# Query, key and value projections: Strassen in float32 replaced by three float32r passes over exact digits

## Chip, cores and metric

The kernel runs on one core of one Trainium2 chip. The metric is device time in microseconds (us) from the first to the last instruction of the core, as the median of several executions of the same program. Engines are named as the profile names them: PE (TensorE, matmuls), PEld (its weight loads), DVE (VectorE), ACT (ScalarE), POOL (GpSimd) and SP (SyncE, which here only issues transfers).

## What is computed

Four sequences of 512 tokens with 1024 features, all in float32. Layer norm, then causal attention with 16 heads and rotary positions, then a gated layer whose weights are signs and whose in- and out-scales are mixed by a router over eight experts; the two are multiplied and added to the input.

```python
x = hidden_states                                  # (4, 512, 1024)
xn = layernorm(x)
q, k, v = xn @ Wq, xn @ Wk, xn @ Wv                # each 1024 x 1024, 16 heads of 64
q, k = rotary(q), rotary(k)
attn = softmax(causal(q @ k.T) / 8)
s = (attn @ v) @ Wo
routing = softmax(xn @ gate_w.T)                   # 8 experts
o = ((xn * (routing @ in_scale)) @ sign(weight).T) * (routing @ out_scale) + bias
out = x + s * silu(o)
```

## The kernel before

**Stages.** The main part goes through the four sequences ("batches") in turn. A batch has four groups of heads; one group is two units, and a unit is two heads (128 rows of Q and K). `projections(b)` is a generator that yields after each matmul of Q, K and V. `interleave` draws from it between the pieces of the attention of the group before, so that TensorE always has a projection matmul to do while softmax runs elsewhere. Then a tail does the last attention, the gated layer and the output projection for eight pairs of token tiles. TensorE's order is the program's order; the other engines are ordered by a scheduler from the data they depend on, but for calls that are pinned. Every engine and every transfer queue runs its own list in order.

**Projections (lines 249 to 498).** `keys` lists ten weight sets a batch: query and key of four groups, and values of two groups at a time. Each set is a 2x2 block product and is done by Strassen with seven products instead of eight: `project_qk` and `project_v` multiply sums of weight quarters (`form_w`, on DVE) with sums of quarters of the normalized, transposed input (`form_x`, on DVE), all in float32 with 256 columns a matmul (L338 for Q and K, L425 for V). V comes out with tokens on the partitions, Q and K with features there. Results are put together by ACT (copies out of the accumulators), DVE (L352, L389, L451) and POOL (L388, L478). `load_w` fetches the next weights, 1 MB a transfer, on SP's queue, into three buffers. `rotary` takes four copies on ACT, one operation on DVE and two on POOL for each unit of Q and K.

**Input.** `load_x`, `half_statistics`, `deviation` and `normalize` do the layer norm of a tile of 128 tokens; `transpose_x` turns it on TensorE (L200) and copies it to `X[b]` on ACT or DVE; the turned tile also goes to device memory (`xn_d`) for the tail. At the start, before the first group, the four tiles of batch 0 go through this one after the other, with projection matmuls between them.

**Router (L629).** `router(b, 0)` multiplies the 32 padded columns of the gate weights with all four token tiles: for each of eight chunks, four matmuls go to four different column groups of the array. Later steps do the softmax over experts.

**Attention.** `scores` (L525), `softmax` (DVE maxima and masks, ACT exponentials with sums, POOL scaling at L561), `transpose_blocks` (ten block transposes on DVE, then 16 moves of 80 KB on SP's queue, L589), `values` (L604, with a copy on ACT and a transfer to `at_d`).

**Around it.** `load_sign` and `make_sign` make the sign weights in four of the groups, from staging tiles of the pool `xin`. `load_scales` and `split_scales` do the same for the expert scales. In batch 3 the first pairs of the tail are prepared on the score banks: `in_scales(0)`, `in_scales(1)` and `out_scales(0)`. The tail's two-part products of the gated layer (`ffn`, L1011, and `gated_by_strassen`, L1180) already use float32r operands: each activation is split into a high and a low part, the signs are exact.

Of the kernel before, what the change touches and what calls it, by code (L numbers as in the profile page):

```python
# [35 lines left out]

# [6 lines left out]
def attn_gated_ffn_kernel(  # L43
# [3 lines left out]
    wqk: bass.AP,  # L47
    wv: bass.AP,
# [16 lines left out]
    sgp = ctx.enter_context(tc.tile_pool(name="sign", bufs=1))  # L65
# [48 lines left out]
    rt_d = dp.tile([B, TPB, 32, P], F32, name="rt_d")  # L114

    sg = {n: sgp.tile([P, E], F32R, name=f"sg{n}") for n in range(NC - 1)}
# [5 lines left out]
    xip = ctx.enter_context(tc.tile_pool(name="xin", bufs=2))  # L122
# [14 lines left out]
    fp = left(name="forms", bufs=1)  # L137
# [14 lines left out]
    X, xin = {}, {}  # L152

    X1 = xp.tile([P, TPB, E], F32, tag="X", name="x_0")

    def load_x(b, t):
        if b == 0:
            xt = X1[:, t, :]
        else:
            xt = xip.tile([P, E], F32, tag="x", name=f"x_{b}_{t}")  # L160
        nc.sync.dma_start(out=xt, in_=x[(b * TPB + t) * P : (b * TPB + t + 1) * P, :])
        xin[b, t] = xt
# [30 lines left out]

    def transpose_x(b, t, g):
        if b not in X:
            X[b] = xp.tile([P, NC, S], F32, tag="X", name=f"X_{b}")
        tp = tp_bank(f"xtp_{b}_{t}_{g}")
        for j in range(4):
            c = 4 * g + j
            nc.tensor.transpose(tp[:, j, :], xin[b, t][:, c * P : (c + 1) * P], ident)  # L200
        dst = X[b][:, 4 * g : 4 * g + 4, t * P : (t + 1) * P]

        if (g == 0 and b > 0) or (g == 1 and (b, t) == (0, TPB - 1)):
            nc.vector.tensor_copy(dst, tp)
        else:
            nc.scalar.copy(dst, tp)
        if g == 1:

            queue = nc.scalar if (b, t) == (B - 1, TPB - 1) else nc.sync
            queue.dma_start(  # L210
                out=xn_d[b, t].rearrange("p (c q) -> p c q", c=NC),
                in_=X[b][:, :, t * P : (t + 1) * P],
            )


    W, Q, K, V = {}, {}, {}, {}
    groups = [(b, g) for b in range(B) for g in range(NGRP)]


    keys = [  # L220
        (b, g, m)
        for b in range(B)
        for g, m in ((0, 0), (0, 1), (1, 0), (1, 1), (0, 2), (2, 0), (2, 1), (3, 0), (3, 1), (2, 2))
    ]

    def load_half_w(key, i):
        if i == 0:
            W[key] = wp.tile([P, 2, NC, P], F32, tag="w", name="w_%d_%d_%d" % key)
        nc.sync.dma_start(
            out=W[key][:, i].rearrange("p c n -> p (c n)"),  # L230
            in_=wqk[key[1], key[2]][:, i * E : (i + 1) * E],
        )


    waiting = [(key, i) for key in keys for i in range(2) if key[2] == 2 or i == 0]

    def load_w():

        if not waiting:
            return  # L240
        key, i = waiting.pop(0)
        b, g, m = key
        if m < 2:
            W[key] = wp.tile([P, 2, NC, P], F32, tag="w", name=f"w_{b}_{g}_{m}")
            nc.sync.dma_start(out=W[key].rearrange("p i c n -> p (i c n)"), in_=wqk[g, m])
        else:
            W[key, i] = wp.tile([P, NC, 2 * P], F32, tag="w", name=f"w_{b}_{g}_{m}_{i}")
            nc.sync.dma_start(
                out=W[key, i].rearrange("p c n -> p (c n)"), in_=wv[g // 2, i]
            )  # L250

    SF, TF = {}, {}

    def quarters_w(key):
        if key[2] < 2:
            w = W[key]
            return w[:, 0, :4, :], w[:, 0, 4:, :], w[:, 1, :4, :], w[:, 1, 4:, :]  # L260
        w, v = W[key, 0], W[key, 1]
        return w[:, :4, :], w[:, 4:, :], v[:, :4, :], v[:, 4:, :]

    def quarters_x(b):
        t = X[b]
        return t[:, :4, :TH], t[:, :4, TH:], t[:, 4:, :TH], t[:, 4:, TH:]

    def form_w(key, n):
        a11, a12, a21, a22 = quarters_w(key)
        values_too = key[2] == 2  # L270


        if n == 1:
            f = a21
        elif values_too and n != 3:
            f = a11 if n == 2 else a21
        else:
            cols = 2 * P if n == 3 else P
            f = fp.tile([P, 4 * cols], F32, tag=f"S{n}", name="S%d_%d_%d_%d" % (n, *key))
            f = f[:, : 4 * (2 * P if values_too else P)].rearrange("p (c n) -> p c n", c=4)  # L280
        SF[key, n] = f
        x0, x1, op = {
            1: lambda: (a21, a22, ALU.add),
            2: lambda: (SF[key, 1], a11, ALU.subtract),
            3: lambda: (a11, a21, ALU.subtract),
            4: lambda: (a12, SF[key, 2], ALU.subtract),
        }[n]()
        nc.vector.tensor_tensor(f, x0, x1, op=op)

    def form_x(b, n):  # L290
        b11, b12, b21, b22 = quarters_x(b)
        if n > 1:
            f = fp.tile([P, 4, TH], F32, tag=f"T{n}", name=f"T{n}_{b}")
        elif b < B - 1:

            f = sgp.tile([P, 4, TH], F32, tag="last", name=f"T1_{b}")
        else:

            f = b12
        TF[b, n] = f  # L300
        if b == B - 1 and n == 2:

# [1124 lines left out]
```

## Time and profile before

| | |
|---|---|
| median of 3 runs | 1108.79 us (1107.62 to 1110.38) |
| the profiled execution, span | 1108.7 us |
| instructions | 15895 |
| mean granted TensorE clock | 0.996 |
| transfers | 163.88 MB, mean 148 GB/s |
| main part (four batches) | from 12.5 to 775.7 us |
| tail | from 775.7 us to the end |

The profile is one execution. A group's row gives line, engine and operation, then what it writes and reads with sizes and count; after the bar, busy time and the mean of one in ns; after the second bar, the engine's idle time just before, and what ended it. In the timeline a row is start, length, engine and group, with neighbours of one kind merged. Matmuls overlap in the pipeline, so a matmul's own length is longer than the distance at which matmuls follow each other.

### The profile page before, as it was taken

The numbers are of one execution on the slowest core, as the hardware profiler recorded it, in microseconds if no ns is written. First come the engines' busy times: TensorE is split into PE (matmuls) and PEld (weight loads), VectorE is DVE, ScalarE is ACT, GpSimd is POOL, SyncE is SP. The second block draws the span as 40 slices with busy tenths as digits, with TensorE's granted clock in tenths as the row PEclk, the third lists the DMA queues.
The fourth block names the chain that finished last, engine by engine and source line by source line (L and its number), as shares of the span: only waits on it lengthen the run. The fifth ranks groups of instructions, "written<-read, shape, count | busy, mean of one in ns | idle before, by whom it ended". The sixth has DMA issues, their size and how long they took to land. (4 is left out here: it accounts for less than half of the span.)

```text
span 1108.7 us, 15895 instructions
## 1 busy us (share of the span) xinstructions
PE 1087.4 (98%) x5176; PEld 790.2 (71%) x5176; DVE 870.4 (79%) x1740; ACT 461.3 (42%) x1072; POOL 518.9 (47%) x566
## 2 busy tenths in 40 slices
PE   9999999999999999999999999999999999999997
PEld 8887778777777877777788687777664545654663
DVE  7888888788988978888887887887776877567663
ACT  2452754453375445427544452655530223122220
POOL 0772645555264555526453562675552433432334
PEclk9999999999999999999999999999999999999999
DMA  9415566544556654455666445544664222431331
GB/s 323 135 69 147 149 184 189 160 137 119 166 155 187 190 154 135 121 163 158 184 183 219 140 148 142 153 125 122 179 193 171 90 93 102 148 119 54 136 114 57
DMA packets 86770, 163.88 MB, mean 148 GB/s; under 512 B 13472, under 2 KB 49056, under 8 KB 80672
## 3 DMA queue, kind: packets, MB, share of 16 engines
q1 hardware_dynamic: 80144, 152.25, 46.1%
q0 software_dynamic: 4832, 9.05, 2.4%
q10 hardware_dynamic: 1712, 1.57, 0.5%
q8 instruction: 41, 0.67, 0.3%
q14 instruction: 41, 0.34, 0.1%
HBM read 95.45 MB, written 25.43 MB: 109 GB/s over the span
## 5 line engine op out<-in xcount | busy, mean ns | idle before, releaser
L561 POOL TENSOR_SCALAR p<-p,rs 128x256 f32<-128x256 f32 (+3 forms) x256 | 183.7, 734 | 200.6 <-DVE rs L559 136.2
L551 ACT ACTIVATE p<-sc,nmx 128x256 f32<-128x256 f32 (+3 forms) x256 | 132.9, 529 | 104.8 <-DVE nmx L548 87.2
L338 PE MATMUL pj<-X,w 128*128 128x256 f32 x576 | 134.3, 382 | 1.7 <-ACT p L551 1.5
L338 PE MATMUL pj<-T,S 128*128 128x256 f32 x512 | 120.5, 385 | 8.5 <-ACT v L613 8.5
L579 DVE STREAM_TRANSPOSE y<-p 128x256 f32<-128x256 f32 x320 | 112.4, 409 | 18.3 <-POOL p L561 16.9
L322 POOL TENSOR_TENSOR sw<-sw,sin_sb 128x512 f32<-128x512 f32 x64 | 85.1, 1330 | 81.1 <-ACT sw L320 75.4
L338 PEld LDWEIGHTS pj<-X,w 128*128 128x128 f32 x576 | 108.1, 190 | 20.0 <-issue 2.9
L338 PEld LDWEIGHTS pj<-T,S 128*128 128x128 f32 x512 | 96.7, 192 | 24.8 <-ACT v L613 11.3
L319 ACT ACTIVATE sw<-c 32x512 f32<-32x512 f32 x128 | 80.3, 628 | 70.0 <-DVE c L352 68.2
L338 PE MATMUL pj<-T,w 128*128 128x256 f32 x448 | 106.6, 382 | 0.0
L548 DVE TENSOR_REDUCE nmx<-sc 128x1 f32<-128x256 f32 (+3 forms) x160 | 105.2, 683 | 1.3
L425 PE MATMUL pj<-w,X 128*128 128x256 f32 x416 | 94.6, 380 | 0.8 <-ACT p L551 0.5
L338 PEld LDWEIGHTS pj<-T,w 128*128 128x128 f32 x448 | 83.4, 190 | 15.5 <-issue 4.6
L323 POOL TENSOR_TENSOR rot<-rot,sw 128x512 f32<-128x512 f32 x64 | 90.8, 1419 | 5.0
L425 PEld LDWEIGHTS pj<-w,X 128*128 128x128 f32 x416 | 78.2, 190 | 12.7 <-ACT p L551 2.0
L545 DVE TENSOR_TENSOR sc<-sc,mask 128x256 f32<-128x256 f32 (+1 forms) x160 | 57.0, 371 | 35.3 <-PE sc L525 35.3
L320 ACT ACTIVATE sw<-c 32x512 f32<-32x512 f32 x128 | 80.4, 628 | 1.6
L425 PE MATMUL pj<-w,T 128*128 128x256 f32 x352 | 80.2, 381 | 0.0
L525 PE MATMUL sc<-rot,rot 64*128 64x128 f32 (+3 forms) x512 | 79.7, 443 | 0.3 <-DVE v L451 0.3
L604 PE MATMUL pv<-p,v 128*64 128x256 f32 (+3 forms) x512 | 76.0, 439 | 0.4 <-issue 0.4
L388 POOL TENSOR_TENSOR part<-part,part 128x256 f32<-128x256 f32 x32 | 24.7, 771 | 105.2 <-ACT part L387 102.0
L613 ACT COPY v<-pv 128x512 f32<-128x512 f32 x32 | 18.7, 585 | 131.5 <-PE pv L604 131.4
(177 smaller groups left out, 1956.9 us busy)
## 6 DMA issues: line engine op xcount, KB each, us to landing
p<-y SPq DMA_DIRECT2D x496, 80.0 KB, 2.1
w<-in_wqk SPq DMA_DIRECT2D x31, 1024.0 KB, 5.3
w<-in_wv SPq DMA_DIRECT2D x16, 1024.0 KB, 5.2
x<-in_x SPq DMA_DIRECT2D x16, 512.0 KB, 4.3
at_d<-v SPq DMA_DIRECT2D x32, 256.0 KB, 2.7
xp<-xn_d SPq DMA_DIRECT2D x16, 512.0 KB, 4.6
ap<-at_d SPq DMA_DIRECT2D x16, 512.0 KB, 5.1
xr<-in_x SPq DMA_DIRECT2D x32, 256.0 KB, 3.0
```

The source lines that it names most:

```text
L319: nc.scalar.activation(sw[r : r + 32, :], c[r + 32 : r + 64, :], AF.Copy, scale=sc)
L320: nc.scalar.activation(sw[r + 32 : r + 64, :], c[r : r + 32, :], AF.Copy, scale=sc)
L322: nc.gpsimd.tensor_tensor(sw, sw, sin_sb, op=ALU.mult)
L323: nc.gpsimd.tensor_tensor(rot, rot, sw, op=ALU.add)
L338: nc.tensor.matmul(ps, lhsT=wq[:, k, :], rhs=xq[:, k, :], start=(k == 0), stop=(k == 3))
L425: nc.tensor.matmul(ps[:, j, :], lhsT=xq[:, k, j * P : (j + 1) * P], rhs=wq[:, k, :], start=(k == 0), stop=(k == 3),)
L525: nc.tensor.matmul(head(i, h), lhsT=Q[u][r : r + D, i * P : (i + 1) * P], rhs=K[u][r : r + D, : (i + 1) * P], start=True, stop=True,)
L548: nc.vector.tensor_reduce(nmx[:, hs], v, AX.X, ALU.max, negate=True)
L551: nc.scalar.activation(pt[:, h, :], ps[h], AF.Exp, bias=nmx[:, h : h + 1], accum_out=ssum[:, h : h + 1],)
L561: nc.gpsimd.tensor_scalar(pt[:, h, :], pt[:, h, :], rs[:, h : h + 1], 1.0, op0=ALU.mult, op1=ALU.mult,)
L579: nc.vector.transpose(out[:, :, :, o : o + 32], src.rearrange("p h (b c) -> p h b c", b=4))
L604: nc.tensor.matmul(by_block[r : r + D, :, 32 * j :], lhsT=V[u][:, j, r : r + D], rhs=PT[u][:, :, o : o + 32 * (TPB - j)], start=(j == 0), ...
```

## The change

Strassen goes. For each of 24 weight sets a batch (Q, K and V of each of the eight units, 128 columns each) the input and the weight are split into two digits of about 12 bits, so that products of digits are exact in float32r: `xh`, `xl` for the input, `hi`, `low` for the weight, where `low` is scaled by 2^12. Three passes give the product: hi with xh, low with xl, and (hi - low) with (xl - xh/2^12), Karatsuba's mixed pass; the sum is formed from two accumulators by ACT (`part_of`) and one DVE operation (`c`). Each pass is eight matmuls of 512 columns (L335 of the changed kernel).

- Weight digits are made in batch 0 (`digits_w`): high digit on ACT, low digit on DVE, its scaling on ACT, the mixed digit on POOL. The raw weight of 512 KB sits in one staging buffer. Both digits, 1 MB, are written to device memory (`w_d`) on SP's queue. In batches 1 to 3 the digits are loaded from there by a transfer that POOL issues, and only the mixed digit is made, on DVE or POOL.
- Input digits are made in `transpose_x` (high digit and a raw copy on ACT) and `low_x` (DVE); `mixed_x` (DVE, four parts) runs at the turn of a batch. The three digit arrays take the place of `X` and the Strassen sums.
- V now comes out by features like Q and K, and is turned by four TensorE transposes a unit (`turn_values`), copied by ACT.
- The raw turned tile of batches 1 to 3 has one buffer (`RAW`), so the router runs tile by tile (`router_tile`): eight chunks into one column group, then the next tile later.
- The input tiles, scales and the first pair of the tail share one fixed tile (`XIN`); sign staging uses `RAW`, and signs are made two a group in batch 3. `out_scales(0)`, `in_scales(1)` and `load_xn(1)` move from batch 3 into the tail.
- At the start, all of layer norm and transposing of batch 0 comes before the first projection matmul; the whole router of batch 0 comes first of all.
- The scratch memory for transfers issued by POOL is set to 8192.

```diff
-    X, xin = {}, {}
+    XH, XL, XM, xin = {}, {}, {}, {}
...
+        hi, _ = digits_of(b, t, g)
+        nc.scalar.activation(hi, tp, AF.Copy, scale=KEEP)
+        nc.scalar.copy(raw_x(b, t)[:, 4 * g : 4 * g + 4, :], tp)
+        if b > 0:
+            low_x(b, t, g)
...
+    def low_x(b, t, g):
+        hi, lo = digits_of(b, t, g)
+        nc.vector.tensor_tensor(lo, TP[b, t, g], hi.bitcast(F32), op=ALU.subtract)
+
+    def mixed_x(b, n):
...
+        at = slice(2 * n, 2 * n + 2)
+        nc.vector.scalar_tensor_tensor(
+            XM[b][:, at, :], XH[b][:, at, :].bitcast(F32), -LOW, XL[b][:, at, :].bitcast(F32),
+            op0=ALU.mult, op1=ALU.add,
+        )
...
-        for g, m in ((0, 0), (0, 1), (1, 0), (1, 1), (0, 2), (2, 0), (2, 1), (3, 0), (3, 1), (2, 2))
+        for g in range(NGRP)
+        for m, i in ((0, 0), (1, 0), (0, 1), (1, 1), (2, 0), (2, 1))
...
+    def load_w(pos):
...
+        WH[key] = wp.tile([P, 2, NC, P], F32R, tag="w", name=f"w_{un}")
+        WM[key] = wp.tile([P, NC, P], F32R, tag="wm", name=f"wm_{un}", bufs=2)
+        if b == 0:
+            WR[key] = tmp.tile([P, NC, P], F32, tag="raw", name=f"wr_{un}", bufs=1)
+            nc.sync.dma_start(out=WR[key].rearrange("p c n -> p (c n)"), in_=wqkv[g, m, i])
+        else:
+            nc.gpsimd.dma_start(out=WH[key].rearrange("p h c n -> p (h c n)"), in_=w_d[g, m, i])
...
+    def digits_w(pos, step):
...
+        hi, low = WH[key][:, 0], WH[key][:, 1]
+        if b == 0:
+            if step == 0:
+                nc.scalar.activation(hi, WR[key], AF.Copy, scale=KEEP)
+            elif step == 1:
+                (nc.vector if pos else nc.gpsimd).tensor_tensor(
+                    low, WR[key], hi.bitcast(F32), op=ALU.subtract
+                )
+            elif step == 2:
+                nc.scalar.activation(low, low.bitcast(F32), AF.Copy, scale=1.0 / LOW)
+        if step == 3:
+            e = nc.gpsimd if b == 0 or m == 2 or (m, i) == (1, 1) else nc.vector
+            e.tensor_tensor(WM[key], hi.bitcast(F32), low.bitcast(F32), op=ALU.subtract)
+            if b == 0:
+                nc.sync.dma_start(out=w_d[g, m, i].bitcast(F32), in_=...)
...
+    def turn_values():
+        while turned:
+            u, c = turned.pop(0)
+            vt = tp_bank("vt_%d_%d_%d" % u)
+            for t in range(TPB):
+                nc.tensor.transpose(vt[:, t, :], c[:, t * P : (t + 1) * P], ident)
+            V[u] = qk.tile([P, TPB, P], F32, tag="v", name="v_%d_%d_%d" % u, bufs=6)
+            nc.scalar.copy(V[u], vt)
...
+        def beside(n):
+            if n == 2:
+                load_w(pos + 2)
+            if n == 5 and turn:
+                rotary(*turn.pop(0))
+            if n == 7:
+                turn_values()
+            if keys[min(pos + 2, len(keys) - 1)][0] == 0:
+                if n in (14, 17, 20, 23):
+                    digits_w(pos + 2, (14, 17, 20, 23).index(n))
+            elif n == 17:
+                digits_w(pos + 2, 3)
...
+        if last:
+            order = [(mixed, xm[b])], [(hi, xh), (low, xl)]
+        else:
+            order = [(hi, xh), (low, xl)], None
+        for _ in passes(first, order[0]):
+            yield
+            n += 1
+            beside(n)
+        p = part_of(un, first, None if last else 1.0 + LOW)
+        second = bank_of(un, 1)
...
+    def router_tile(b, t):
...
+        for c in range(NC):
+            nc.tensor.matmul(lg[rows, :], lhsT=gw[:, c, :], rhs=raw_x(b, t)[:, c, :],
+                start=(c == 0), stop=(c == NC - 1))
+        nc.scalar.copy(R[b][rows, :], lg[rows, :])
```

## The prediction

> **What bounds the kernel now.** I read the busy shares first, then the stages, then what TensorE waits for, then the start-to-start distance of its matmuls.
>
> ```profile
> PE 1087.4 (98%) x5176; PEld 790.2 (71%) x5176; DVE 870.4 (79%) x1740; ACT 461.3 (42%) x1072; POOL 518.9 (47%) x566
> ...
> 12.50:193.70 181.20, 178.92 (x947) 145.81 (x948) 154.31 (x312) 88.69 (x205) 91.21 (x97) 1.00 0.54 162
> 193.70:387.20 193.50, 191.43 (x1028) 150.68 (x1027) 164.94 (x360) 95.97 (x234) 98.23 (x109) 1.00 0.55 159
> 387.20:583.50 196.30, 193.47 (x1091) 152.28 (x1090) 165.25 (x361) 96.23 (x235) 100.29 (x112) 1.00 0.56 159
> 583.50:775.70 192.20, 188.05 (x950) 147.35 (x950) 155.59 (x355) 91.63 (x229) 98.77 (x113) 0.99 0.52 148
> 775.70:1108.60 332.90, 324.80 (x1094) 183.79 (x1093) 223.64 (x340) 85.15 (x162) 128.56 (x125) 0.99 0.37 121
> ```
>
> The windows are the four batches and the tail (columns: window, length, busy time of PE, PEld, DVE, ACT, POOL, granted clock, DMA share, GB/s). TensorE is the bound in every stage, at full clock. DVE is second, at 85% of each batch; ACT and POOL are half free. TensorE's longest wait in total is "PE pj L338 <- ACT v L613: 8.5, 7, 2.3" of the wait list, so nearly nothing is left to win but TensorE's own work.
>
> ```profile
> 743.47 1.89 PE L338 MATMUL pj<-T,w 128*128 128x256 f32 x8
> ...
> 879.65 0.39 PE L1180 MATMUL ff<-sg,lo_a 128*128 128x512 f32 x1
> ...
> 881.47 0.39 PE L1180 MATMUL ff<-sg,lo_a 128*128 128x512 f32 x1
> 881.69 0.40 PE L1180 MATMUL ff<-Tsg,hi_S 128*128 128x512 f32 x1
> ...
> 883.79 0.40 PE L1180 MATMUL ff<-Tsg,lo_S 128*128 128x512 f32 x1
> ...
> 11.23 1.06 PE L200 MATMUL xtp<-ident,x 128*128 128x128 f32 x8
> ...
> 18.40 1.95 PE L629 MATMUL lg<-X,gw 128*32 128x128 f32 x64
> ```
>
> Durations overlap, so starts count. A float32 matmul is two instructions: eight of 256 columns take 1.89, less the last one's 0.38, over seven: 0.216 us each. A float32r matmul of 512 columns (the trace calls it f32; hi and lo tiles are float32r) is one instruction: between the first two ff lines lie eight steps, 1.82/8 = 0.2275 us, between the last two nine, 2.10/9 = 0.2333. So it does twice the columns of such an instruction, and needs one where float32 needs two. Transposes go at (1.06-0.27)/7 = 0.113. The router's 64 matmuls take 1.95 us, because four column groups run together: 0.11 per four.
>
> **The change on TensorE.** Strassen has 7x4 matmuls of 256 columns for each of 8 query and key sets, 7x8 for each of 2 value sets: 336 a batch, 1344, 2688 instructions, at 0.216 = 580.6 us. The new form has 24 sets a batch, 3 passes of 8 chunks: 2304 instructions. Between the two ff distances I take 0.230: 529.9 us, so **-50.7**. Ends: 0.2275 gives -56.4, 0.2333 gives -43.1; at the 0.216 of the float32 row, the lowest there is, -82.9. [...]
>
> Values now come out by column and are turned: 32 units x 4 transposes x 0.11 = **+14.1**. The router is now computed a token tile at a time, eight chunks in the same column group one after the other, so its four groups no longer run together: 256 instructions x 0.109 = 27.9, instead of 16 x 4 x 0.11 = 7.0: **+20.9** (if neighbours overlapped after all, 0). TensorE's account is therefore only -15.7.
>
> **The start.** Now QKV is fed between the transposes from 12.53 on; when the router ends at 20.3, 16 of its instructions (3.5 us) are done. Afterwards all four tiles must be through first. Each tile costs ACT four copies of 0.59 and DVE 1.3 (statistics), 0.2, 0.15, 0.81 and two low digits of 0.69, in turns: normalized slabs at about 7.6, 12.6, 17.9 and 22.1. ACT has the high digit of key 1 ahead of the last copies, which waits for its load (staging buffer free at 19.4, landed 24): copies end at 27.5, the router's last tile at 30.1. So QKV starts at 30.1 with 7.0 of router before it, against (20.3-3.5) with 1.95: 23.1-14.9 = **+8.2** (5 to 12).
>
> **Batch 0 must make its weight digits.** Per key: load 512 KB into one staging buffer, high digit (ACT), low digit (DVE), scaling (ACT), mixed digit (POOL), 1 MB to device memory (SP). The next load waits until the low digit has read the only buffer.
>
> ```profile
> L1153 ACT CAST hi_a<-xp 128x512 fp32r<-128x512 f32 x18 | 10.5, 617 | 32.9 <-issue 17.8 <-DVE xp L1150 9.1 <-DVE xp L763 6.0
> ...
> L288 DVE TENSOR_TENSOR w<-w 128x1024 f32<-128x1024 f32 x16 | 21.9, 1366 | 1.6 <-PE pj L425 1.4
> ...
> L322 POOL TENSOR_TENSOR sw<-sw,sin_sb 128x512 f32<-128x512 f32 x64 | 85.1, 1330 | 81.1 <-ACT sw L320 75.4 <-DVE mv L177 5.1 <-PE pj L338 0.3
> ...
> x<-in_x SPq DMA_DIRECT2D x16, 512.0 KB, 4.3
> ...
> 499.67 4.39 SPq L589 DMA_DIRECT2D p<-y  x7
> ```
>
> The shortest round is load 4.3, high digit 0.617 + 512 columns at 0.85 ns (exp: 689 ns for 512, 364 for 128) = 1.05, low digit 1.37, SP's issue 0.35: 7.1 us. TensorE's round in groups 1 to 3 is 24 x 0.230 = 5.5 plus 2.2 for attention, transposes and router (batch 0's 181.2 less 145.2 of QKV and 4.3 of start, plus 3.5 for turned values and 3.9 for three router tiles, over 18 keys): 7.7. The two are near, and nothing else is slack: per key ACT needs 7.05 (two digits 2.1, part 0.59, rotary 4 x 0.628 on two keys of three, softmax 4.15 per unit of three keys, copies of x and v), DVE 6.9, POOL 6.5 (2.66 for the mixed digit). Queues run in order, so a high digit stands behind exps and a low digit behind ten block transposes (4.1 us). On SP the 16 block moves of a unit take 16 x 0.63 = 10 us of issuing, and in the built order of SP weight loads stand behind them. I add 1.0 for ACT, 0.7 for DVE, 0.7 for SP: 9.5 a round, **+32** over 18 keys; group 0, walked the same way from 30.1, waits 1.4 at key 4 and at key 5: **+35**. Ends: 0 if the round stays below 7.7, +63 at 11.
>
> **Batches 1 to 3.** What goes: all sums of quarters on DVE. DVE falls below today's share, ACT too. What comes: 72 loads of 1 MB issued by POOL, half the mixed digits on POOL (36 x 2.66 = 96 us in all), the mixed digits of x, four of about 1.6 us on DVE at each turn of batch; they lie beside the last key's 16 and the next key's 16 matmuls (7.4 us). If that cover fails, up to 6.5 a batch. A load is asked for two keys ahead, about 15 us, and takes 5.3 (the 1 MB w rows); POOL may be 10 us late before anyone waits.
>
> ```profile
> p<-y SPq DMA_DIRECT2D x496, 80.0 KB, 2.1
> ...
> p<-y POOLq DMA_DIRECT2D x8, 80.0 KB, 3.5
> ```
>
> POOL's queue is slower for the same move (3.5 against 2.1), and the load stands behind softmax scalings that wait for reciprocals. I take **+7**; ends 0 and +40. [...]
>
> **Tail.** The out-scales of pair 0 and the in-scales of pair 1, until now in batch 3 on the score banks, move behind the first scores of the tail and onto the four ring banks; ffn's next bank waits for four ACT copies (2.4) behind eight exps (today os already waits 2.0 for exp). The last values wait for part and sum, 1.3, before they are turned. **+6.5** (0 to 10).
>
> Sum: -50.7+14.1+20.9+8.2+35+7+6.5 = +41 on the profiled 1108.7: **1149.7**, say 1149; the profiled execution equals the median, 1108.79.
>
> **Rivals.** *TensorE alone decides (faster).* Slack counts for it: ACT and POOL are half free, and TensorE hardly waits today. With 0.2275, no lost round in batch 0, the start at +5, the tail at +2: -56.4+14.1+20.9+5+2 = -14, **1094**. It decides as long as the weight round stays under 7.7 us. Against it: 7.1 without any queueing. *Even.* The same with 0.230, start 8.2, tail 6.5: -1, **1108**. *POOL's queue stops the later batches too.* Each load 0.6 us late beyond its cover on 72 keys: +43 on the forecast, **1192**. For it: POOL waits for DVE (136 us) and for block moves (64) at L561 today, and the loads now stand behind that. It decides once a load comes more than the 10 us of lead late. Against: that lead. *The passes aren't single*: two instructions per float32r matmul would add 2304 x 0.23 = 530 us; the ff rows are one each, so under 1%.
>
> **Chances.** Forecast (1118 to 1172) 0.47, POOL's queue 0.23, faster 0.22, even 0.08. This kernel's measurement can't tell less than 0.3% (3.3 us) from no change. Of the even case 0.06 falls within that bound and 0.02 above it, so: faster 0.22, same 0.06, slower 0.47+0.23+0.02 = 0.72. The range takes in the gain of a free batch 0 and most of POOL's case: 1096 to 1195.
>
> **What would show it.** Distance of QKV matmuls 0.2275 to 0.2333; router 7 us a batch; first QKV matmul at 30; batch 0 at about 225 us long with TensorE waiting at L335 for low or mixed digits, and batches 1 to 3 near 193. If batch 0 is under 200 us, the round is hidden and I am wrong; if batches 1 to 3 exceed 200 us, POOL's rival holds.

## The result, and the profile after

The changed kernel takes 1240.62 us (median of 4 runs, 1237.91 to 1242.54) against 1108.2 (1107.45 to 1110.38) for the kernel before on the same chip: ratio 1.1185, 95% interval [1.1161, 1.1208]. The profiled execution took 1237.91 us with a span of 1236.2. The forecast was 1149, range 1096 to 1195.

First the busy row and the clock row of the page, then the stages (window, length, busy time of PE, PEld, DVE, ACT and POOL, granted clock, DMA share, GB/s): start, four batches, tail.

```profile
PE 1115.1 (90%) x4928; PEld 763.9 (62%) x4928; DVE 866.1 (70%) x1498; ACT 573.0 (46%) x1223; POOL 647.3 (52%) x651
...
PEclk9989899899999999899999989898989999999999
```

```profile
12.50:30.90 18.40, 11.12 (x97) 10.12 (x96) 14.88 (x19) 10.95 (x21) 5.52 (x3) 0.91 0.69 227
30.90:263.30 232.40, 189.08 (x848) 139.70 (x848) 141.29 (x245) 146.96 (x265) 135.46 (x111) 0.92 0.63 211
263.30:473.40 210.10, 194.29 (x964) 141.68 (x963) 156.75 (x290) 112.85 (x264) 123.49 (x132) 0.98 0.71 208
473.40:682.70 209.30, 191.61 (x964) 139.76 (x963) 155.70 (x288) 111.57 (x260) 122.63 (x132) 0.98 0.69 202
682.70:892.40 209.70, 189.30 (x891) 137.01 (x889) 160.32 (x296) 101.34 (x243) 128.65 (x132) 0.94 0.65 194
892.40:1236.20 343.80, 330.61 (x1109) 186.74 (x1108) 230.68 (x353) 85.34 (x165) 129.73 (x129) 0.98 0.37 125
```

TensorE is no longer busy all the time, and it no longer has its full clock (0.962 in the mean, 0.996 before). All batches are longer, not only batch 0, which makes the digits; and no engine is at its limit: DVE, second before, is less busy than it was. So the time is in waits. TensorE's (waiting line, releaser, us in total, times, longest):

```profile
PE pj L335 <- ACT w L274: 21.3, 5, 6.0
PE sc L419 <- DVE c L379: 18.4, 5, 7.2
PE vt L318 <- DVE c L379: 16.9, 13, 5.3
PE pj L335 <- ACT p L445: 14.6, 6, 4.1
PE xtp L210 <- DVE x L187: 9.2, 3, 5.2
PE vt L318 <- DVE c L375: 7.7, 4, 3.8
PE pj L335 <- ACT part L310: 7.1, 6, 1.6
PE vt L318 <- DVE rs L453: 5.4, 4, 2.2
```

Two families stand out: the digits of batch 0 (high digits `w` of ACT), and everything that hangs on DVE's sum `c` of the two halves of a projection: the turn of the values (`vt`) needs `c` itself, the scores (`sc`) need a PSUM bank that is free once `c` has read it. No line names a weight load (`w_d`): POOL's loads came in time. The rest are mainly waits for ACT (exponentials `p`, copies `part`) and three waits of the start (`xtp`).

A stretch of batch 0 shows what a wait costs (start, duration of the group, instruction, tile, count, idle time before):

```profile
118.00 2.00 PE L335 MATMUL pj<-xl,w 128*128 128x512 f32 x8
119.83 1.97 PE L335 MATMUL pj<-xm,wm 128*128 128x512 f32 x8
127.81 3.36 PE L335 MATMUL pj<-xh,w 128*128 128x512 f32 x7 [6.00 <-ACT w L274]
...
131.82 1.98 PE L335 MATMUL pj<-xl,w 128*128 128x512 f32 x8
133.63 1.98 PE L335 MATMUL pj<-xm,wm 128*128 128x512 f32 x8
```

Between the last two rows lie eight matmuls: (133.63-131.82)/8 = 0.226 us each. The seven behind the wait of 6.0 us take (130.96-127.81)/7 = 0.45 each (the next instruction of TensorE starts at 130.96): the clock is halved (0.50 granted), from 124.5 to 131.3 by the clock record. There are 20 such stretches in the trace, 96.5 us in all; before there were 3, 11.9 us.

That gives an account. Idle time between matmuls (with the 1.5 us before the first) went from 15.6 to 116.6 us, +101.0. Half clock, at 0.45 us a matmul in place of 0.226, costs at most half of its time: (96.5-11.9)/2 = +42.3. What is left of the span, the work at full clock, went from 1087.1 to 1071.4: **-15.7**. This last term is a remainder, so the three give the difference of the spans, 127.5, by construction. And one part is counted twice: in the half-clock stretches TensorE had no matmul for 16.9 us (3.0 before), and that time is idle time already. Counted once, half clock costs about 35 us, and the work fell by about 8. Either way TensorE's work fell by little, and idle time and clock took it back many times over.

### The profile page after: what moved, and what is told of

Its sections match the earlier page's. It is cut to its first block, busy times and chain, and to the rows that moved or that the text cites. A ratio compares the mean times of both kernels' runs of the same rounds, so it can differ in the third digit from the quotient of the medians.

```text
span 1236.2 us, 15609 instructions
## 1 busy us (share of the span) xinstructions
PE 1115.1 (90%) x4928; PEld 763.9 (62%) x4928; DVE 866.1 (70%) x1498; ACT 573.0 (46%) x1223; POOL 647.3 (52%) x651
## 4 chain that ended last, share of the span: by engine, by line
PE 48%; DVE 20%; ACT 11%; issue 8%; POOL 6%; DMA 6%; SPq 1%; DVEq 0%; POOLq 0%; ACTq 0%
PE pj L335 16%; PE wo L1139 14%; PE ff L1079 5%; ACT p L445 4%; DVE y L473 4%; PE pv L498 3%; PE sc L419 3%; DVE rot L297 3%; DMA wr<-in_wqkv 2%; POOL p L455 2%; DVE nmx L442 2%; DVE wm L283 2%; DVE c L379 2%; PE ff L908 2%; PE lg L524 2%
## 5 line engine op out<-in xcount | busy, mean ns | idle before, releaser
L335 PE MATMUL pj<-xh,w 128*128 128x512 f32 x768 | 214.0, 417 | 43.0 <-ACT w L274 21.3
L335 PE MATMUL pj<-xl,w 128*128 128x512 f32 x768 | 208.4, 405 | 0.9 <-ACT w L280 0.9
L335 PE MATMUL pj<-xm,wm 128*128 128x512 f32 x768 | 203.0, 404 | 5.3 <-ACT v L507 3.0
L335 PEld LDWEIGHTS pj<-xh,w 128*128 128x128 f32 x768 | 150.6, 200 | 81.5 <-ACT w L274 23.4
L283 POOL TENSOR_TENSOR wm<-w 128x1024 fp32r<-128x1024 f32 x60 | 148.0, 2467 | 63.1 <-ACT w L280 55.9
L335 PEld LDWEIGHTS pj<-xm,wm 128*128 128x128 f32 x768 | 147.5, 195 | 41.4 <-issue 7.6
L335 PEld LDWEIGHTS pj<-xl,w 128*128 128x128 f32 x768 | 144.8, 193 | 41.8 <-issue 11.9
L419 PE MATMUL sc<-rot,rot 64*128 64x128 f32 (+3 forms) x512 | 82.9, 447 | 18.4 <-DVE c L379 18.4
L379 DVE TENSOR_TENSOR c<-pj,part 128x512 f32<-128x512 f32 x92 | 62.0, 674 | 45.5 <-PE pj L335 37.4
L297 DVE SCALAR_TENSOR_TENSOR rot<-c,cos_sb 128x512 f32<-128x512 f32 x64 | 90.9, 1420 | 1.3
L283 DVE TENSOR_TENSOR wm<-w 128x1024 fp32r<-128x1024 f32 x36 | 45.0, 1249 | 65.0 <-PE pj L335 58.1
L419 PEld LDWEIGHTS sc<-rot,rot 64*128 64x128 f32 x512 | 43.7, 188 | 49.6 <-issue 20.9
```

The source lines that it names most:

```text
L283: e.tensor_tensor(WM[key], hi.bitcast(F32), low.bitcast(F32), op=ALU.subtract)
L297: nc.vector.scalar_tensor_tensor(rot, c, sc, cos_sb, op0=ALU.mult, op1=ALU.mult)
L335: nc.tensor.matmul(ps, lhsT=wd[:, k, :], rhs=xd[:, k, :], start=(at == 0), stop=(at == n - 1),)
L379: nc.vector.tensor_tensor(c, second, p, op=ALU.add)
L419: nc.tensor.matmul(head(i, h), lhsT=Q[u][r : r + D, i * P : (i + 1) * P], rhs=K[u][r : r + D, : (i + 1) * P], start=True, stop=True,)
```

## The experiments

Thirteen kernels were run. Stage lengths run from the first QKV matmul of a batch to that of the next; idle is the time between matmul records (with the 1.5 us before the first), half the length of the half-clock stretches (the last one reaches up to 2 us past the end), and "rest" = span - idle - half/2. The stages are those of the profiled execution.

| kernel | median us | ratio to before [95%] | batch 0 | batches 1-3 | tail | idle | half | rest |
|---|---|---|---|---|---|---|---|---|
| before | 1108.2 | | 181 | 194 196 192 | 333 | 15.6 | 11.9 | 1087 |
| changed | 1240.6 | 1.1185 [1.1161, 1.1208] | 232 | 210 209 210 | 344 | 116.6 | 96.5 | 1071 |
| e1 turn later | 1214.0 | 1.0958 [1.0896, 1.1019] | 227 | 199 203 203 | 345 | 95.8 | 91.0 | 1068 |
| e2 no digits | 1207.4 | 1.0899 [1.0867, 1.0930] | 199 | 212 212 216 | 338 | 100.9 | 75.9 | 1068 |
| e3 loads by SP | 1235.0 | 1.1148 [1.1089, 1.1208] | 231 | 209 211 205 | 343 | 113.7 | 104.3 | 1065 |
| e4 fillers | 1263.2 | 1.1403 [1.1370, 1.1436] | 242 | 215 215 214 | 341 | 56.1 | 69.8 | 1171 |
| e5 no mixed digit | 1171.1 | 1.0538 [1.0517, 1.0559] | 226 | 193 195 185 | 337 | 70.2 | 67.0 | 1066 |
| e6 raw loads by ACT | 1218.3 | 1.0954 [1.0929, 1.0979] | 210 | 212 215 209 | 344 | 102.7 | 113.0 | 1065 |
| e7 mixed stored | 1192.4 | 1.0741 [1.0716, 1.0766] | 234 | 195 198 191 | 343 | 86.8 | 77.8 | 1070 |
| e8 router by chunk | 1237.9 | 1.1144 [1.1122, 1.1166] | 228 | 210 212 211 | 342 | 113.6 | 99.9 | 1070 |
| e9 four edits | 1165.8 | 1.0497 [1.0447, 1.0548] | 219 | 194 191 191 | 344 | 74.1 | 51.9 | 1068 |
| e10 mixed by DVE | 1203.2 | 1.0848 [1.0828, 1.0868] | 230 | 199 199 199 | 340 | 89.6 | 80.2 | 1072 |
| e11 mixed by POOL | 1223.6 | 1.1037 [1.1016, 1.1058] | 229 | 203 204 206 | 342 | 101.3 | 100.2 | 1067 |
| e13 e9, no POOL mixed | 1158.3 | 1.0442 [1.0422, 1.0462] | 215 | 193 192 185 | 341 | 65.4 | 44.3 | 1068 |

The last column supports the account: 1065 to 1072 in every changed version without fillers (1068 to 1077 if idle time at half clock is counted once). Whatever an edit moved, it moved idle time and clock, hardly the work.

**e1: the values turned later.** A key's values are turned during the next key, after 7 of its 24 matmuls, so part, sum and turn have 7 x 0.227 = 1.6 us of cover.

```
-            if n == 7:
+            if n == 14:
                 turn_values()
```

> The values' transposes are put after the 14th matmul of the next weight set instead of the 7th. In the changed kernel TensorE waits 30 us in total before these transposes. Theory A (each new wait in TensorE's order costs by itself, and the clock gate adds to it): these waits fall under 8 us and the time falls by 20 to 35 us, to 1205 to 1220. Rival B (DVE is simply late, and whatever TensorE asks of it next waits instead): the waits move to the next bank or scores and the time stays within 8 us of 1240.

Measured: 1213.96. The waits of `vt` fell from 30.0 to 7.4 us, batches 1 to 3 from 210 to between 199 and 203. The place of the turn alone is worth 27 us.

**e2: no digits at all.** Every batch loads the raw weights twice in place of the digits; neither high, low and scaled digits nor their copy in device memory are made. POOL issues the raw loads in batch 0 too, and half of batch 0's mixed digits move to DVE, as in the other batches.

```
+        for h in range(2):
+            nc.gpsimd.dma_start(out=WH[key][:, h]..., in_=wqkv[g, m, i])
...
-        if b == 0:
+        if False:
             if step == 0:
                 nc.scalar.activation(hi, WR[key], AF.Copy, scale=KEEP)
```

> Left out: making the weight digits and writing them to device memory; every batch loads the raw weight into both halves of the digit tile (two transfers of 512 KB issued by POOL), so batch 0 runs like the others and the product is not the reference's. Theory A (the one staging buffer's round sets batch 0): batch 0 falls from 232 us to 200 to 212, no wait of TensorE on the digit operations is left, batches 1 to 3 stay near 210, total 1205 to 1220. Rival B (ring banks and turned values set batch 0 too): batch 0 stays above 220.

Measured: 1207.4. Batch 0 fell by 33.5 us to 199; batches 1 to 3 did not fall, they rose by 2 to 6. So the digits of batch 0, with their loads on SP's queue, are worth about what the forecast gave them (+35), and the rest of the loss, 99 us, remains without them.

**e3: the digit loads on SP's queue.** This is the rival that the forecast named: loads that stand behind POOL's work.

```
-            nc.gpsimd.dma_start(out=WH[key]..., in_=w_d[g, m, i])
+            nc.sync.dma_start(out=WH[key].bitcast(F32)..., in_=w_d[g, m, i].bitcast(F32))
```

> Batches 1 to 3 load their digits on SP's queue instead of POOL's. POOL stands idle 84 us before these issues, waiting for TensorE to free the weight buffer, with softmax scalings behind it. Theory C (that blocking makes probabilities, DVE and so TensorE late): batches 1 to 3 fall by 5 to 12 us each, total 1205 to 1225. Rival A (waits come from how close TensorE's order puts its consumers): under 5 us of change in all. If SP's 16 block moves ahead of a load make weights late, TensorE waits for w and the time grows.

Measured: 1235.02, 6 us less, with intervals that overlap. The waits of the scores went, and a new one came:

```profile
PE pj L335 <- DMA w<-w_d: 41.4, 15, 6.2
PE pj L335 <- ACT w L274: 20.4, 5, 5.5
```

Behind SP's block moves the loads are late; on POOL they were not. Yet POOL's queue may have had a part in the trouble: with POOL's arithmetic all in place the waits of the scores went, the waits of `vt` fell to 6.9 us, and DVE's operation `rot` took 1086 ns in the mean in place of 1420. The 41.4 us of new waits also spread the work out, so this run doesn't say how much was the queue. In e5, e7 and e10 below the loads stay on POOL, and the waits of the scores (nearly) go as well.

**e4: fillers against the clock.** Transposes without use are put ahead of the turn (14) and, in batch 0 from the sixth key on, ahead of each weight set (27), 961 in all.

```
+            for _ in range(14):
+                nc.tensor.transpose(vt[:, 0, :], ident, ident)
...
+        if 4 < pos < 24:
+            for _ in range(27):
+                nc.tensor.transpose(first[:, :P], ident, ident)
```

> Added: 14 dummy transposes (1.5 us) before each unit's turned values, and 27 (3.0 us) before each weight set of batch 0 from the sixth on: 32 x 1.5 + 19 x 3.0 = 105 us of TensorE work, put where it waits today (some 60 us). Theory A (the half-rate windows, 92 us of them against 7 before, come from these gaps): half-rate time falls under 40 us, and the time is 1238 + 105 - 60 - 30 = about 1250. Rival B (the gate follows something else): half-rate time stays near 90 and the time is about 1283.

Measured: 1263.24. The work grew by 100 us, but idle time fell by 60.5 and half-clock time by 26.7, to 69.8. That is between theory A (under 40) and theory B (near 90); 17 us of it lie ahead of the first QKV matmul, where no filler was added and the changed kernel had 3.4. In batch 0, where the fillers cover the waits, no stretch is at half clock (37.5 us in the changed kernel). In batches 1 to 3, where no filler covered the waits of the scores (22.1 us in all), each batch still had 10 to 24 us at half clock. So the half clock follows the waits, and is no effect of the float32r passes. As a remedy it is too dear.

**e5: without the mixed digit.** Why is `c` late in batches 1 to 3, where DVE has less to do than before? A stretch there, rows of DVE and POOL from their timelines:

```profile
502.04 0.87 DVE L553 TENSOR_TENSOR rex<-rex,rrs 128x32 f32<-128x32 f32 x1
...
503.65 4.21 DVE L561 TENSOR_TENSOR rex<-rex,rhi 128x32 f32<-128x32 f32 x2
504.09 2.38 POOL L283 TENSOR_TENSOR wm<-w 128x1024 fp32r<-128x1024 f32 x1
...
506.44 1.26 POOL L298 TENSOR_TENSOR sw<-sw,sin_sb 128x512 f32<-128x512 f32 x1
...
507.78 4.13 DVE L565 COPY rex<-rhi 128x32 f32<-128x32 f32 x2
508.29 1.28 POOL L299 TENSOR_TENSOR rot<-rot,sw 128x512 f32<-128x512 f32 x1
509.52 2.35 POOL L283 TENSOR_TENSOR wm<-w 128x1024 fp32r<-128x1024 f32 x1
...
511.83 3.37 DVE L473 STREAM_TRANSPOSE y<-p 128x256 f32<-128x256 f32 x10
515.13 0.65 DVE L379 TENSOR_TENSOR c<-pj,part 128x512 f32<-128x512 f32 x1
```

Two subtractions of 32 columns take 4.21 us, two copies 4.13; the pair takes 0.29 and 0.30 at 723.86 in the same trace, where POOL is idle. Each ends about when POOL's run of tensor operations does: the long one of each pair, 4.11 and 4.02 us, 0.05 us after it. The transposes and the next `c` stand behind them, TensorE's scores behind that `c`: they go on at 515.83, after a wait of 5.04 us.

```
-            e = nc.gpsimd if b == 0 or m == 2 or (m, i) == (1, 1) else nc.vector
-            e.tensor_tensor(WM[key], hi.bitcast(F32), low.bitcast(F32), op=ALU.subtract)
...
+        mixed = low
```

> The mixed weight digit is left out (no subtraction on POOL or DVE; the third pass multiplies the scaled low digit), so the output is not the reference's. Theory A: POOL's 2.4 us tensor operations on whole tiles hold up VectorE's operations on tiles beside them (a 128x32 subtraction of 0.17 us took up to 4.1 us in the changed kernel, rot up to 5.6), that makes the sums c late, and TensorE waits for the banks or the turn. Then VectorE's time above the shortest of each kind falls from 137 us to under 100, rot's mean from 1.42 to under 1.0 us, the waits of the scores for banks (18.4 us) go, batches 1 to 3 come to 198 to 205 each, and the total is 1200 to 1218 (about half of the gain from the clock that is halved less often). Theory B: c is late only because of its place in VectorE's queue behind ten block transposes; rot stays above 1.3 us, less than 8 us are won: 1230 or more.

Measured: 1171.12, 69 us less than the changed kernel, more than theory A gave. Batches 1 to 3 take 193, 195 and 185, the waits of the scores are gone, and DVE's time above the shortest of each kind (for each line, tile and shape, what its operations take beyond the value that a tenth of them stay under) falls from 137 to 67 us; it is 82 in the kernel before. But this takes 45 us of work from DVE as well as 148 from POOL, so e7, e10 and e11 part the two.

**e7: the mixed digit stored and loaded.**

```
-        if step == 3:
-            e = nc.gpsimd if b == 0 or m == 2 or (m, i) == (1, 1) else nc.vector
-            e.tensor_tensor(...)
+        if step == 3 and b == 0:
+            nc.gpsimd.tensor_tensor(...)
...
+                nc.gpsimd.dma_start(out=wm_d[g, m, i], in_=WM[key]...)
...
                 load_w(pos + 2)
+                load_mixed(pos + 1)
```

> The mixed digit is stored too in batch 0 and loaded in batches 1 to 3 (72 loads of 512 KB more on POOL's queue) in place of the subtraction, of which 36 were on POOL at 2.4 us and 36 on VectorE at 1.25. Theory A (POOL's tensor operations hold up VectorE): batches 1 to 3 fall from 210 to 198 to 205, rot's mean there under 1.0 us, total 1205 to 1222. Theory B (transfers and POOL's queue decide there): the additional 36 MB and 72 issues of 0.6 us give it back, weights come late and TensorE waits for DMA: 1232 to 1260.

Measured: 1192.35, better than expected by A. With 72 loads more on POOL's queue the batches are shorter. TensorE waits 6.9 us in all for the new loads.

**e10 and e11: the mixed digits all on one engine.**

```
-            e = nc.gpsimd if b == 0 or m == 2 or (m, i) == (1, 1) else nc.vector
+            e = nc.gpsimd if b == 0 else nc.vector            (e10)
+            e = nc.gpsimd                                     (e11)
```

> In batches 1 to 3 all 72 mixed digits are made by VectorE: 36 operations of 2.4 us leave POOL, 36 of 1.25 us (45 us of work) come to VectorE. Theory A (what costs time is POOL's long operations that hold up VectorE): rot's mean falls from 1.42 to about 1.1 us, VectorE's time above the shortest of each kind from 137 to about 95, total 1200 to 1228. Theory B (what costs time is VectorE's own work, the 36 mixed digits it already has): VectorE gets later, c too; total 1245 to 1265.

> The other way: in batches 1 to 3 all 72 mixed digits are made by POOL: 36 operations of 1.25 us leave VectorE, 36 of 2.4 us come to POOL (about 85 us). Theory A: more of VectorE's operations are held up; the time above the shortest of each kind goes from 137 to 160 or more, the total does not fall and may rise: 1236 to 1270. Theory B: VectorE is relieved of 45 us: 1215 to 1230.

Measured: 1203.18 and 1223.61. The rows of `rot` (busy us in all, mean ns of one), in the kernel before, in the changed kernel, in e10 and in e11:

```profile
L321 DVE SCALAR_TENSOR_TENSOR rot<-c,cos_sb 128x512 f32<-128x512 f32 x64 | 45.3, 734 | 0.2
```

```profile
L297 DVE SCALAR_TENSOR_TENSOR rot<-c,cos_sb 128x512 f32<-128x512 f32 x64 | 90.9, 1420 | 1.3
```

```profile
L297 DVE SCALAR_TENSOR_TENSOR rot<-c,cos_sb 128x512 f32<-128x512 f32 x64 | 59.3, 926 | 1.2
```

```profile
L297 DVE SCALAR_TENSOR_TENSOR rot<-c,cos_sb 128x512 f32<-128x512 f32 x64 | 93.9, 1467 | 1.3
```

In e10 DVE gets 36 operations more and is busy for less: 849.6 us against 866.1, for its time above the shortest falls from 137 to 83. The waits of the scores go from 18.4 to 1.4. That is theory A; theory B's 1245 us or more are far off. e11 came out where theory B had it (1215 to 1230), a miss for A: 36 more operations on POOL did not make it slower but 17 us faster. The hold-up did grow as A says, the time above the shortest from 137 to 153, and the waits of the scores stayed (18.6); but DVE has 45 us less to do, and the waits for the turn fall from 30 to 19. So both count: the waits of the scores follow the hold-up, those of the turn partly DVE's own load. The split between both engines was the worst of the three.

**e12: the two engines by themselves.** A kernel of its own, outside the computation: VectorE's kinds of operation alone, then beside six POOL subtractions of 128x1024.

```
+    for v, nv, p, np_ in ((stt, 12, None, 0), (tt, 12, None, 0), (tt_psum, 12, None, 0), ...
+                          (None, 0, p_tt, 6), (stt, 12, p_tt, 6), (tt, 12, p_tt, 6), ...
+        nc.vector.tensor_tensor(r0, d[:, :8], g[:, :8], op=ALU.add)
+        nc.gpsimd.tensor_tensor(r1, r0, r1, op=ALU.add)
+        for _ in range(np_): p()
+        for _ in range(nv): v()
```

> A kernel of its own that computes nothing of the reference: VectorE's kinds of operation, 12 of 512 columns each, first alone, then beside six POOL subtractions of 128x1024 (2.4 us each), then beside POOL's scalings of 384 columns and beside POOL's loads. Theory A (POOL's tensor operations hold up VectorE's when those read two SBUF operands or copy): scalar_tensor_tensor and tensor_tensor from SBUF go from about 0.68 us alone to well above it beside POOL, single ones to 2.4 us and more; the sum with a PSUM operand (c: 0.68 in every run) and the block transpose stay as alone. Theory B (no such thing; the long operations of the changed kernel are late operands): every kind takes the same beside POOL as alone within 10%.

DVE's timeline (start, length of the whole row of operations). First alone:

```profile
6.03 8.69 DVE L78 SCALAR_TENSOR_TENSOR vd<-va,vb 128x512 f32<-128x512 f32 x12
...
15.03 8.68 DVE L81 TENSOR_TENSOR vd<-va,vb 128x512 f32<-128x512 f32 x12
...
24.02 8.67 DVE L87 TENSOR_TENSOR vd<-ps,va 128x512 f32<-128x512 f32 x12
...
32.99 5.50 DVE L90 COPY vd<-va 128x512 f32<-128x512 f32 x12
...
38.79 4.12 DVE L93 STREAM_TRANSPOSE vd<-va 128x128 f32<-128x128 f32 x12
...
43.22 5.39 DVE L84 TENSOR_TENSOR vd<-va,vb 128x32 f32<-128x32 f32 x24
...
63.78 20.95 DVE L78 SCALAR_TENSOR_TENSOR vd<-va,vb 128x512 f32<-128x512 f32 x12
...
85.04 20.95 DVE L81 TENSOR_TENSOR vd<-va,vb 128x512 f32<-128x512 f32 x12
...
106.29 8.67 DVE L87 TENSOR_TENSOR vd<-ps,va 128x512 f32<-128x512 f32 x12
...
121.19 17.76 DVE L90 COPY vd<-va 128x512 f32<-128x512 f32 x12
...
139.26 4.12 DVE L93 STREAM_TRANSPOSE vd<-va 128x128 f32<-128x128 f32 x12
...
154.13 17.69 DVE L84 TENSOR_TENSOR vd<-va,vb 128x32 f32<-128x32 f32 x24
```

The rows from 63.78 on are those beside POOL. Operations with two SBUF inputs, and the float32 copy, gain 12.3 us in each case, whatever their length: 8.69 to 20.95, 5.50 to 17.76, 5.39 to 17.69. POOL's six alone take 14.4, so it looks as if the engines took turns: 20.95 us is nearly the sum of both times, 23.1. With one input in PSUM (the form of `c`) and in a block transpose nothing changes, 8.67 and 4.12. That is theory A, kind by kind: `c` is never slow itself, it stands behind operations that are. Beside POOL's scalings of 384 columns twelve operations took 11.33; beside its DMA issues 8.68, as alone, but only two issues fell into that time, so this says little.

**e6: batch 0's raw loads on ACT's queue.** The wait of 6.0 us above ends with a high digit. Here are SP's queue ahead of it, and ACT:

```profile
108.85 11.50 SPq L483 DMA_DIRECT2D p<-y  x16
120.45 0.52 SPq L285 DMA_DIRECT2D w_d<-w  x1
121.07 8.31 SPq L259 DMA_DIRECT2D wr<-in_wqkv  x2
```

```profile
126.70 1.06 ACT L274 ACTIVATE w<-wr 128x1024 fp32r<-128x1024 f32 x1 [6.01 <-DMA wr<-in_wqkv]
```

The load waited in SP's queue for the 16 moves of a unit.

```
-            nc.sync.dma_start(out=WR[key]..., in_=wqkv[g, m, i])
+            (nc.scalar if pos > 1 else nc.sync).dma_start(out=WR[key]..., in_=wqkv[g, m, i])
```

> In batch 0 the raw weight loads are issued by ACT's queue and no longer by SP's. Theory A: TensorE's waits for the high digits (21.3 us) come from loads that stand behind the 16 block moves of a unit on SP (11.5 us of issuing); then ACT's wait for the load (23.4 us, 10 times) falls under 6, batch 0 shrinks from 232 to 205 to 212, and the total is 1208 to 1220. Theory B: the round of one staging buffer (load 3.7, high 1.06, low 1.23 and their waits) is too long on any queue; batch 0 stays over 222 and the total over 1228.

Measured: 1218.26; batch 0 takes 209.5, 23 us less, and the waits for the high digit are no longer in TensorE's list. The queue was the cause of these waits, not the length of a round with one buffer.

**e8: the router of batch 0 by chunk.**

```
-            for t in range(TPB):
-                router_tile(b, t)
+            for c in range(NC):
+                for t in range(TPB):
+                    nc.tensor.matmul(lg[32 * t : 32 * t + 32, :], lhsT=gw[:, c, :], rhs=raw_x(b, t)[:, c, :], ...)
```

> Batch 0's router runs chunk by chunk over the four token tiles again, as in the kernel before, so the four column groups alternate: 7.0 us should become about 2. Theory A: the router stands on the path ahead of the first QKV matmul; it starts 4 to 5 us earlier (25.5 to 27) and the total falls by 3 to 6: 1234 to 1238. Theory B: batch 0 waits for its weight digits anyway and takes the gain back: QKV starts earlier, but the total stays within 1238 to 1243.

Measured: 1237.91 against 1240.62, the intervals of the ratios overlap ([1.1122, 1.1166] and [1.1161, 1.1208]). QKV started at 29.4 in place of 30.9; the expected 4 to 5 us were not there, since the 64 matmuls took 4.4 us here and 5.96 in the changed kernel (1.95 in the kernel before). The clock record shows why 4.4: half clock from 25.9 to 29.3, nearly all of this router; the changed kernel's had full clock. No verdict beyond "small".

**e9 and e13: together.** e9 joins e1, e6, e7 and e8; e13 also makes batch 0's mixed digits on VectorE. The edit from e9 to e13:

```
-            nc.gpsimd.tensor_tensor(WM[key], ...)      (e9)
+            nc.vector.tensor_tensor(WM[key], ...)      (e13)
```

> Four edits together: the mixed digit stored and loaded (alone 1192), raw weight loads of batch 0 on ACT's queue (alone 1218), the chunk-by-chunk router of batch 0 (alone 1238) and the values turned at matmul 14 of a key (alone 1214). If the four act on different waits: 1240.6 - 48 - 22 - 3, and of the turn's 27 only some 8, for most of its waits went with the mixed digit: about 1160, 1150 to 1175, batches 1 to 3 at 190 to 195, batch 0 at 205. Rival: the gains are partly the same idle time of batch 0, which only moves from one wait to the next: 1180 or more. Neither expects it under the kernel before.

> The four edits together (1166 before), and batch 0's 24 mixed digits on VectorE too, so POOL makes none. Theory A (the hold-up is what is left of batch 0's 35 us idle time): batch 0 falls from 219 to 205 to 212, the total to 1150 to 1160. Theory B (batch 0 waits for VectorE's own queue: low digits, sums, router's scales): 24 x 1.25 = 30 us more work on it, batch 0 stays or grows: 1163 to 1180.

Measured: 1165.83 and 1158.33, both where the first theory had them, though batch 0 fell less than they said (219 in e9, not 205; 214.5 in e13, not 205 to 212), and the intervals of the two ratios overlap a little. The longest wait left in batch 0 of e9, 8.6 us for a `c`, stands behind a `rot` of 4.70 us beside POOL and behind the splitting of the scales (1.00, 2.27 and 2.17 us on DVE): the hold-up is part of it, DVE's own queue probably the other. The stages of e13, batches 0 to 3 and the tail:

```profile
30.80:245.30 214.50, 183.02 (x848) 136.22 (x848) 162.70 (x275) 145.87 (x269) 100.93 (x114) 0.95 0.86 293
245.30:438.20 192.90, 187.29 (x963) 138.86 (x962) 118.32 (x276) 112.10 (x261) 103.00 (x144) 1.00 0.99 290
438.20:629.80 191.60, 187.30 (x963) 138.87 (x962) 118.24 (x275) 111.97 (x261) 102.66 (x144) 1.00 0.99 287
629.80:814.60 184.80, 178.43 (x891) 130.62 (x889) 129.85 (x287) 99.38 (x239) 109.90 (x142) 1.00 1.01 289
814.60:1155.40 340.80, 326.24 (x1110) 184.47 (x1108) 230.26 (x349) 85.53 (x166) 129.70 (x129) 0.99 0.38 127
```

Batches 1 to 3 are now 569 us at full clock, 13 less than before: 0.6, 4.7 and 7.4 us. In batch 3 part of it is no gain, since preparations of the tail moved out of it; so what this version keeps of the passes' gain is at most some 4 us a batch. But QKV starts 18 us later, batch 0 is 33 longer and the tail 8, so the best version that was run is still 4.4% slower than the kernel before. The DMA share of 0.99 suggests that the next limit in these batches may be near. A version that gives the product without making digits in batch 0 was not tried.

## Why the prediction was wrong, step by step

The direction was right, the size was not: the profiled run took 1237.9, 88 us over the sum of 1149.7. By stages the sum had start and batch 0 together at 193.7 - 12.7 + 3.5 + 5.2 + 8.2 + 35 = 232.9 (measured 263.3), batches 1 to 3 together at 582 - 38 + 10.6 + 15.7 + 7 = 577 (629.1) and the tail at 339.4 (343.8). So 30 us of the miss lie in start and batch 0, 52 in batches 1 to 3 and 4 in the tail.

- **TensorE's passes, -50.7: a little better.** One instruction each, 0.226 us in place of 0.230. The rival of two instructions is out.
- **Turned values +14.1 and router +20.9: work about as forecast.** 16 router matmuls in a row take 1.93 us (four times that is 7.7 for a batch, 7.0 forecast), the first 64 took 5.96. That the sum with the passes, -15.7, equals the remainder of the account to the tenth is luck: by these distances and rows alone it would be about -24, and the remainder is about -8 once idle time at half clock is counted once. What fills the gap is not known.
- **Start +8.2: right here, with luck.** First QKV matmul at 30.9, forecast 30.1. In e1, e5, e7, e10 and e11, which start the same way, it came at 32.7 to 34.7, with 10 to 17 us at half clock ahead of it in place of 3.4; the forecast had no such term.
- **Batch 0 +35: nearly right for the waits, half right in cause.** Its idle time rose by 41 and e2 gives the digits 33.5; the half clock, up to 19 us, came on top and was not in the sum. TensorE's waits were for high digits (21.3 us), not for low or mixed ones (1.2) as the forecast had it. And SP's block moves, for which the forecast added 0.7 us a key, were the larger part: 23 us went with e6. The forecast's own row of these moves (4.39 for 7) held the price; it was spread evenly over the keys when it strikes one key in three with the whole 11.5 us.
- **Batches 1 to 3, +7: the step that failed.** The term measured +59 (629.1 against 570 without it); idle time there rose by 44.9 us. The text set "half the mixed digits on POOL" beside other work at no cost, and it checked POOL's and DVE's totals apart. They are not apart: DVE's operations with two inputs in SBUF, and its copies, wait out most of POOL's (e12: 8.69 us became 20.95, 5.50 became 17.76), which made a DVE with less work later than before. Nor did it price the turn's wait: it named "part and sum, 1.3" for the tail only, not for 32 units with 1.6 us of cover (30.0 us; e1).
- **The clock, never in the sum.** All durations were taken at the full clock that the kernel before had. The half clock cost about 35 us (42 if idle time in it is counted too), some two fifths of the miss. It is no independent cause: it follows the waits (e4), and in e13 the same passes ran through batches 1 to 3 at full clock.
- **Tail +6.5: too low by 4.** It measured +10.9, just outside its 0 to 10: idle time +6.1, half clock +3.

Of the rivals, "POOL's queue stops the later batches too" comes nearest: it gave 43 us of waiting, and batches 1 to 3 do exceed 200, which the forecast took as its sign. Yet its mechanism, late loads, was wrong: no weight load was late until e3 moved the loads away from POOL. It was POOL's arithmetic, which stands in DVE's way; that the loads on its queue decide when this arithmetic runs, and so add to the hold-up, e3 suggests and no run separates. "TensorE alone decides" fell with the first wait.

What the forecast lacked, e12 measured kind by kind: beside six POOL subtractions VectorE's operations went from 8.69 to 20.95 us with two SBUF inputs and from 5.50 to 17.76 for the float32 copy, and stayed at 8.67 with an input in PSUM and at 4.12 for block transposes. What in the chip makes them wait, no run shows.

## What to carry to other kernels

Before work is put on an engine that looks half free, ask whose work it holds up: in e12 six POOL subtractions of 2.4 us added 12.3 us, 2 us each, to VectorE's operations with two SBUF inputs, and the loser may be an operation that stands far behind in that queue, as `c` was here (TensorE waited up to 7.2 us for it). Sum waits at the places where one result has little cover (count the matmuls between producer and consumer), not as averages of a stage; and add to each wait of about 2 us or more on TensorE some 1.7 us for the clock, an estimate from the changed kernel's trace (half of its shortest half-clock stretch, 3.41 us; 7 of the 20 were two or three times as long). Where an edit's gain is some 4 us of work per stage, any new wait of that size per stage decides the outcome.

## What the runs showed of the hardware

- **About 2 us of idle time in TensorE was enough for half clock.** In the traces of both kernels the half-clock stretches of a run start on one fixed grid of 3.413 us and last whole multiples of it (3.413, 6.827 or 10.240 us), up to the last (5.057 us before, 4.385 in the changed kernel). In the changed kernel, after the start, a window of that grid at full clock with 1.91 us or more of idle time was followed by one at half clock every time, with less than 1.8 us in nearly all cases not (three exceptions at 0.67, 1.52 and 1.59; the trace may lack matmuls). In the kernel before 2.01 and 2.34 us were followed by half clock, 1.39 us and less were not. Over the traces of both kernels and the variants, after the start, the bound is not sharp: 1.96 us was once not followed (e4), 2.0 and more always was. A window already at half clock was sometimes followed by another with much less idle time (0.12 to 1.21 us, five times in the changed kernel). So 101 us more of idle time cost some 136, with the 35 us of half clock. It may also be why the same kernel differs by some us between runs (1237.91 to 1242.54 for the changed one); that is a guess and was not tried.
- **POOL's operations hold up VectorE's even at 32 columns**: 24 additions that take 5.39 us alone took 17.69 beside 14.7 us of POOL's work (e12), and a subtraction of 0.18 us took 4.11 in the changed kernel.
